# A two-layer convolution and scan network: the front of layer 0 in a planned order, with part of a depthwise convolution on VectorE

## The chip, the core and the metric

The kernel runs on one core of one Trainium2 chip, in one launch. The core has TensorE (PE in the profile), VectorE (DVE), ScalarE (ACT), GpSimd (POOL) and SyncE (SP); each takes its instructions in its own order, and they meet at semaphores. SP issues nearly all DMAs. The metric is the device time of one execution, in microseconds; lower is better. "Before" is given as the median of three runs.

## The reference

The input is an image of 64 x 64 tokens with 96 channels (L = 4096 tokens). Two layers follow each other, each with a mixer and a small network per token, both added to the residual. The change is in layer 0's mixer alone, cut here to what it touches:

```python
# x: (1, 64, 64, 96); D_INNER = 192, D_STATE = 16, DT_RANK = 6
x = (x - mean(x)) / sqrt(var(x) + 1e-6)              # over the 96 channels
xz = x @ in_proj_w
x_val, z = xz[..., :192], xz[..., 192:]
x_val = silu(depthwise_conv3x3(x_val, conv_w) + conv_b)
s1 = x_val in row order;  s3 = x_val in column order
y = scan(s1) + reversed scan(s1) + scan(s3) + reversed scan(s3)
y = layernorm(y) * silu(z)
return y @ out_proj_w

def scan(u):
    x_dbl = u @ x_proj_w                              # dt, B, C
    dt = softplus(x_dbl[:, :6] @ dt_proj_w + dt_proj_b)
    log_dA = dt * A;  dB_u = dt * B * u
    decay = exp(cumsum(log_dA))
    h = decay * cumsum(dB_u / (decay + 1e-12))
    return sum(h * C) + u * D_skip
```

In layer 0 a scan is alive only near its start: the sums of dt soon make `decay` vanish against 1e-12. So the kernel computes the four scans on their first TE = 160 tokens (the "ends"), adds these to `4 * D_skip * u`, and tests at run time whether anything further on could matter. With this data nothing does.

## The kernel before, in words

All of this lies in `front0` (L417), which ends at a branch at L309, `tc.If(self.alive > 0)`, behind which the full scan stands; it isn't taken. Then come `decays` (eight small loads on SP, L1881 and L1884) and `middle` (L1098), the rest of layer 0 and layer 1, whose order a planner lays out; the first of its instructions on TensorE is L1356.

Tokens are cut into NCH = 8 chunks of CH = 512 (8 image rows each). Channels 0 to 127 are "group 0", channels 128 to 191 "group 1". Images with a border of zeros are kept in `pad`: `pad[0][:, 0]` is the upper half of group 0, `pad[0][:, 1]` its lower half with the two halves of the 128 partitions exchanged, `pad[1]` group 1, once on each half of the partitions. So 64 x 64 diagonal weights, `self.diag` (made on POOL, L385), on the four quadrants of TensorE can take four parts of a depthwise convolution side by side. All diag products are float32.

- `norm_in0` (L440) runs a loop of NCH + 2 rounds in three stages: a chunk's mean and centring on VectorE and square on ScalarE; in the next round the variance, the root on ScalarE, the scaling and four transposes to `xt`; in the round after that the two products of the projection, which go to `pad[0]` by ScalarE (L505) and to `pad[1]` by VectorE (L506). `awake` puts products of the identity with itself between them, 26 at first. Two "edge" rows (L477) are the rows next to the middle line, wanted by the other half.
- After it `prepare0` (two Exps and a Silu on ScalarE) and `mlp_weights` twice: loads on SP and casts on VectorE, the second set in the same memory as the first.
- `conv_ends` (L518) computes the convolution at the ends of the four scans alone, first in row order (o = 0, two turns of 27 products), then in column order (o = 1, 54 and 36); `silu_ends` (L558) puts them into `ue`.
- `x_proj`, `dt_proj`, `log1p` and what follows in `scan_ends` (L688) compute the ends' scans, nearly all on VectorE, with Sigmoid, Exp and the like on ScalarE. `alive` (L855) is their run-time test.
- Beside these runs the list `beside`, one step at each call of `others`: 54 steps of the whole convolution (`conv0`, L589), four products each in four quadrants, with a Silu per finished tile (L608) and its store to `u_d` (SP), and then four steps of the gate silu(z) (`gate0`, L652), whose results go over `pad`. `scaled` (L672) multiplies by 4 D_skip on ScalarE. `add_ends` (L867) adds the ends to `y` on VectorE.

Every instruction here is wrapped in `keep`, so engines run them in the order of the program. `values_load` (L862) has each engine read `alive` before it branches.

`Order` (L141) is the planner of the later stages: operations are added with an engine, a cost, what they read and write, and buffers from named slots; `run` takes the operation that can start first by these costs, of those that can start at once the one with the longest chain behind it plus its `lead`, and emits it:

```python
od.add("DVE", cost, emit, r=[what it reads], w=[what it writes], new={key: slot tag})
```

Of the kernel before, what the change touches and what calls it, by code (L numbers as in the profile page):

```python
# [123 lines left out]
PAIRS = HW // 2  # L124

# [130 lines left out]
class Net:  # L256
    def __init__(self, ctx, tc, x, out):
# [8 lines left out]
        for c in range(NCH):  # L266
            nc.sync.dma_start(self.res[:, c], xv[:, c])
# [149 lines left out]
    def front0(self, wp, w, w1, pad):  # L417
# [5 lines left out]
        with ExitStack() as ctx:  # L423
# [6 lines left out]
            self.norm_in0(wp, lp, pm, pe, xt, pad)  # L430
# [7 lines left out]
            self.add_ends(*self.scan_ends(ep, pm, pe, pad, beside))  # L438

    def norm_in0(self, wp, lp, pm, pe, xt, pad):  # L440

        nc, keep = self.nc, self.keep
        xc, v, t = {}, {}, {}

        def small(name, c):
            return lp.tile([P, 4], F32, tag=name, name=f"{name}a{c}")

        def wide(name, c):
            return lp.tile([P, 4, CD], F32, tag=name, name=f"{name}a{c}")
# [3 lines left out]


        keep(nc.scalar.activation(small("lnr", "x")[:, 0:1], self.eps6, AF.Sqrt))

        warm = pm.tile([P, CH], F32, tag="m", name="warm")

        def awake(products):
            for _ in range(products):  # L460
                keep(nc.tensor.matmul(warm[:, 0:P], self.ident, self.ident, start=True, stop=True))

        awake(26)
        for i in range(NCH + 2):
            new, mid, old = (c if 0 <= c < NCH else None for c in (i, i - 1, i - 2))
            if old is not None:
                t[old] = [pm.tile([P, CH], F32, tag="m", name=f"in0{old}{g}") for g in range(2)]
                for g in range(2):
                    w = self.w_in[:, g * P : (g + 1) * P] if g or old < NCH // 2 else self.w_turned
                    keep(nc.tensor.matmul(t[old][g], w, xt[:, chunk(old)], start=True, stop=True))  # L470
                half = old - NCH // 2 + 1
                if half in (0, 1):

                    edge = pm.tile([P, CH], F32, tag="m", name=f"edge{half}")[:, 0:HW]
                    at = L // 2 - HW * (1 - half)
                    w = self.w_in[:, 0:P] if half else self.w_turned
                    keep(nc.tensor.matmul(edge, w, xt[:, at : at + HW], start=True, stop=True))  # L477
                awake(2 if half not in (0, 1) else 1)
            if mid is not None:
                sq, v[mid] = v[mid], small("lnv", mid)  # L480
                keep(nc.vector.tensor_reduce(v[mid], sq, AX.X, ALU.add))
                keep(nc.scalar.activation(v[mid], v[mid], AF.Sqrt, bias=self.eps6, scale=1.0 / CD))
            if new is not None:
                m, x = small("lnm", new), self.res[:, new]
                keep(nc.vector.tensor_reduce(m, x, AX.X, ALU.add))
                xc[new] = wide("lnxc", new)
                keep(nc.vector.scalar_tensor_tensor(xc[new], spread(m), -1.0 / CD, x, ALU.mult, ALU.add))
                v[new] = wide("lnsq", new)
                keep(nc.scalar.activation(v[new], xc[new], AF.Square))
            if mid is not None:  # L490
                r, xn = small("lnr", mid), wide("lnxn", mid)
                keep(nc.vector.reciprocal(r, v.pop(mid)))
# [3 lines left out]
                for j in range(4):  # L496
                    keep(nc.tensor.transpose(t4[0:CD, j, :], xn[:, j, :], self.ident))
# [11 lines left out]
            if mid is not None:  # L509
                keep(nc.scalar.copy(xt[:, chunk(mid)], tr[0:CD]))  # L510
# [2054 lines left out]
```

## Time and profile before

| | us |
|---|---|
| median of three runs | 1261.97 (1258.34 to 1267.21) |
| the profiled execution, its own time | 1267.05 |
| its span, first to last instruction | 1265.2 |
| norm and projection, until the last L506 ends | 0 to 40.1 |
| products of the ends (L537), first and last | 39.8 to 55.0 |
| first polynomial step on VectorE (L986) | 60.2 |
| last product of conv0 (L639) ends, about | 106.4 |
| `alive` written (L855) | 109.0 |
| first TensorE work behind the branch (L1356) | 122.25 |

The mean granted TensorE clock was 0.871 of full speed over the span. In the stretches that matter:

```profile
core 0: us, PE busy (x) PEld busy (x) DVE busy (x) ACT busy (x) POOL busy (x), PEclk, DMA share, GB/s
0.00:10.00 10.00, 8.24 (x48) 8.25 (x49) 5.07 (x14) 2.72 (x5) 3.37 (x34) 1.00 0.64 185
10.00:40.00 30.00, 28.43 (x149) 19.30 (x149) 19.54 (x41) 14.01 (x30) 7.27 (x15) 1.00 0.08 17
40.00:60.00 20.00, 20.00 (x330) 15.15 (x326) 4.76 (x19) 8.56 (x20) 0.00 (x0) 1.00 0.08 20
60.00:109.00 49.00, 49.00 (x432) 16.81 (x424) 47.09 (x66) 26.99 (x31) 0.00 (x0) 1.00 0.46 135
109.00:122.20 13.20, 9.57 (x30) 2.86 (x28) 3.62 (x17) 8.35 (x12) 0.00 (x0) 0.93 0.19 38
122.20:130.00 7.80, 7.75 (x14) 2.83 (x14) 1.27 (x3) 0.51 (x1) 0.41 (x3) 0.67 0.84 193
```

Each row is a stretch, then its length, then the busy time of the engines in the order PE, PEld (TensorE's weight loads), DVE, ACT, POOL, with the number of instructions; at the end the granted TensorE clock, the busy share of the DMA engines and what they moved. A float32 product leaves two records in the trace. In other lines of the timeline the first number is the start, the second the time from the first to the last of merged instructions, and brackets give the idle time before and what ended it.

### The profile page before, as it was taken

The numbers are of one execution on the slowest core, as the hardware profiler recorded it, in microseconds if no ns is written. First come the engines' busy times: TensorE is split into PE (matmuls) and PEld (weight loads), VectorE is DVE, ScalarE is ACT, GpSimd is POOL, SyncE is SP. The second block draws the span as 40 slices with busy tenths as digits, with TensorE's granted clock in tenths as the row PEclk, the third lists the DMA queues.
The fourth block names the chain that finished last, engine by engine and source line by source line (L and its number), as shares of the span: only waits on it lengthen the run. The fifth ranks groups of instructions, "written<-read, shape, count | busy, mean of one in ns | idle before, by whom it ended". The sixth has DMA issues, their size and how long they took to land.

```text
span 1265.2 us, 11505 instructions
## 1 busy us (share of the span) xinstructions
PE 1042.1 (82%) x3666; PEld 427.2 (34%) x3666; DVE 1138.5 (90%) x922; ACT 884.0 (70%) x1068; POOL 847.7 (67%) x517
## 2 busy tenths in 40 slices
PE   9998988987367788897778877787778889898886
PEld 7632233322122222332222222333223444333434
DVE  6395698577989999999999999999999999999787
ACT  4455566545677878888778877888778878777435
POOL 3000385243277878978888878988888878976566
PEclk9999989997578888888878889898789999888875
DMA  2062110146755665545735675545736766423201
GB/s 74 13 171 77 26 26 13 50 152 209 232 172 158 224 219 196 149 137 178 243 126 157 224 209 206 148 139 175 239 126 196 241 210 222 149 80 93 78 1 51
DMA packets 79134, 183.17 MB, mean 145 GB/s; under 512 B 21534, under 2 KB 34936, under 8 KB 77688
## 3 DMA queue, kind: packets, MB, share of 16 engines
q1 hardware_dynamic: 78376, 182.16, 45.7%
q8 instruction: 31, 0.51, 0.2%
q14 instruction: 39, 0.32, 0.1%
q10 hardware_dynamic: 688, 0.19, 0.1%
HBM read 159.73 MB, written 21.52 MB: 143 GB/s over the span
## 4 chain that ended last, share of the span: by engine, by line
DVE 41%; PE 15%; issue 9%; ACT 4%; DMA 2%; POOL 1%; SPq 0%; another core or an unknown queue 0%; POOLq 0%; DVEq 0%; ACTq 0%
DVE xws L2007 13%; DVE h1s L2007 12%; DVE h0s L2007 7%; PE hs L2018 6%; PE hs L2022 3%; DVE x1s L2007 3%; DVE x0s L2007 2%; DVE x2s L2007 2%; ACT da L1992 2%; ACT xws L1977 1%; DMA kept<-xn 1%; PE acc L2046 1%; POOL hss L2012 1%; DMA x2s<-bc 1%; PE late L2332 1%
## 5 line engine op out<-in xcount | busy, mean ns | idle before, releaser
L2035 POOL TENSOR_TENSOR kept<-kept,kept 128x1024 f32<-128x1024 f32 x92 | 216.9, 2358 | 81.9 <-issue 39.8
L2012 POOL TENSOR_TENSOR hss<-h1s,xws 128x1024 f32<-128x1024 f32 x96 | 228.1, 2378 | 60.0 <-DVE xws L2007 57.2
L2018 PE MATMUL hs<-h0s,ident 128*128 128x512 f32 x360 | 220.1, 697 | 28.0 <-DVE h0s L2007 24.1
L1992 ACT ACTIVATE da<-dt1s,a 128x1024 f32<-128x1024 f32 x168 | 187.5, 1117 | 69.3 <-DVE xws L2007 54.7
L2007 DVE TENSOR_TENSOR_SCAN xws<-da,xws 128x1024 f32<-128x1024 f32 x96 | 222.1, 2313 | 12.4 <-ACT da L1992 12.3
L1992 ACT ACTIVATE da<-dt0s,a 128x1024 f32<-128x1024 f32 x166 | 185.1, 1116 | 39.7 <-DVE h0s L2007 16.1
L2022 PE MATMUL hs<-hss,ident 128*128 128x512 f32 x368 | 189.1, 606 | 21.4 <-POOL hss L2012 21.4
L2007 DVE TENSOR_TENSOR_SCAN h1s<-da,h1s,xws 128x1024 f32<-128x1024 f32 x72 | 167.6, 2328 | 0.8 <-ACT da L1992 0.5
L2046 PE MATMUL acc<-kept,fold 128*32 128x512 f32 x368 | 88.7, 694 | 68.5 <-POOL kept L2035 68.5
L2031 ACT COPY kept<-hs 128x512 f32<-128x512 f32 x184 | 107.1, 582 | 48.5 <-PE hs L2022 47.7
L2018 PEld LDWEIGHTS hs<-h0s,ident 128*128 128x128 f32 x360 | 71.3, 215 | 152.8 <-issue 82.3
L2022 PEld LDWEIGHTS hs<-hss,ident 128*128 128x128 f32 x368 | 69.4, 193 | 120.6 <-issue 78.8
L2018 PE MATMUL hs<-x0s,ident 128*128 128x512 f32 x128 | 73.5, 658 | 13.8 <-DVE x0s L2007 13.8
L2018 PE MATMUL hs<-x1s,ident 128*128 128x512 f32 x128 | 72.4, 650 | 13.4 <-DVE x1s L2007 13.4
L1971 POOL TENSOR_TENSOR x1s<-x1s,dus 128x1024 f32<-128x1024 f32 x32 | 75.5, 2361 | 8.8 <-DMA x1s<-bc 8.8
L2018 PE MATMUL hs<-x2s,ident 128*128 128x512 f32 x120 | 67.5, 646 | 14.5 <-DVE x2s L2007 14.5
L1971 POOL TENSOR_TENSOR x2s<-x2s,dus 128x1024 f32<-128x1024 f32 x32 | 75.8, 2367 | 0.3 <-DMA x2s<-bc 0.3
L2007 DVE TENSOR_TENSOR_SCAN x0s<-da,x0s 128x1024 f32<-128x1024 f32 x32 | 74.0, 2313 | 1.1 <-ACT da L1992 1.1
L2007 DVE TENSOR_TENSOR_SCAN x1s<-da,x1s 128x1024 f32<-128x1024 f32 x32 | 74.0, 2313 | 1.1 <-ACT da L1992 1.1
L2007 DVE TENSOR_TENSOR_SCAN x2s<-da,x2s 128x1024 f32<-128x1024 f32 x32 | 74.1, 2316 | 0.9 <-ACT da L1992 0.7
L1244 POOL MEMSET pairs<- 96x256 f32 x1 | 0.3, 308 | 103.3 <-ACTq L309 103.3
L1977 ACT COPY xws<-x1s 128x1024 f32<-128x1024 f32 x32 | 63.4, 1980 | 5.2 <-POOL hss L2012 5.2
(372 smaller groups left out, 1973.7 us busy)
## 6 DMA issues: line engine op xcount, KB each, us to landing
kept<-bc SPq DMA_DIRECT2D x92, 512.0 KB
x2s<-bc SPq DMA_DIRECT2D x32, 512.0 KB
x0s<-bc SPq DMA_DIRECT2D x28, 512.0 KB
x1s<-bc SPq DMA_DIRECT2D x28, 512.0 KB
dus<-du SPq DMA_DIRECT2D x20, 512.0 KB
dt1s<-dt SPq DMA_DIRECT2D x20, 512.0 KB
dt0s<-dt SPq DMA_DIRECT2D x20, 512.0 KB
kept<-xn SPq DMA_DIRECT2D x24, 384.0 KB
```

The source lines that it names most:

```text
L1244: nc.gpsimd.memset(self.pairs1[:, :, 0 : HW + 2 : HW + 1, :], 0.0)
L1971: keep(nc.gpsimd.tensor_tensor(x, x, du[:, part[j]], ALU.mult))
L1977: keep(copy(grid(xw)[:, w, :], cols(xs[i % 3])[:, w, :]))
L1992: keep(nc.scalar.activation(t, dts[o][:, part[j]], AF.Exp, scale=self.a6[:, g, k : k + 1]))
L2007: keep(nc.vector.tensor_tensor_scan(to, da, x, start, ALU.mult, ALU.add))
L2012: keep(nc.gpsimd.tensor_tensor(cols(hs)[:, w, :], grid(h1)[:, w, :], grid(xw)[:, w, :], ALU.add))
L2018: keep(nc.tensor.matmul(t, self.ident, x[:, chunk(m)], start=k == 0, stop=False))
L2022: keep(nc.tensor.matmul(sums[i, m], self.ident, hs[:, chunk(m)], start=False, stop=True))
L2031: keep(nc.scalar.copy(to, sums.pop((i, j * (SC // CH) + h))))
L2035: keep(nc.gpsimd.tensor_tensor(t, t, times_c_by(i, a), ALU.mult))
L2046: keep(nc.tensor.matmul(to, self.fold4, src, start=k == 0, stop=k == NK - 1))
L2332: keep(nc.tensor.matmul(at["s", a, h], self.ident, t[:, s], start=k == 0, stop=k == 1))
```

## The change

- `norm_in0` is laid out by the planner instead of the three-stage loop. Chunks come in the order 0, 7, 1, ..., 6, and SP loads them in this order. Mean and variance come from VectorE's statistics instruction (two per chunk); the Square on ScalarE and two reductions go. Both copies to `pad` are ScalarE's. Of the products that fill TensorE only the first 26 are left.
- The row-order ends (`conv_ends` with o = 0, tap by tap, and their `silu_ends`) are planned into it too, as soon as chunks 0 and 7 are in `pad`. In the program `silu_ends` then stands ahead of `prepare0`.
- The upper half of group 0 (half of the tokens of 128 channels) leaves TensorE: `upper_tap` computes it on VectorE, in two parts of 16 rows by 64, nine taps each, the first a product with a scalar per channel, the other eight in place: multiply and add. ScalarE's Silu then works in place on `y`.
- `conv0` has 36 steps instead of 54: each is four products, one per quadrant, the lower half of group 0 with group 1. The calls of `others` are moved accordingly, `scaled(0)` is called after 27 steps and the last two gate steps before `yc`.
- `x_proj` scales with ScalarE instead of VectorE.
- 14 products of the identity are put in front of `yc` (L860).

```diff
@@ -122,6 +122,8 @@
+IN_DVE, OTHERS = (), (15, 9, 9)
 BY_SUMS, TIMES_POOL = (0, 1), (0, 3)
@@ -263,7 +265,7 @@
         xv = x.rearrange("(c p j) d -> p c j d", c=NCH, j=4)
-        for c in range(NCH):
+        for c in (0, NCH - 1, *range(1, NCH - 1)):
             nc.sync.dma_start(self.res[:, c], xv[:, c])
@@ -427,7 +429,8 @@
             xt = fp.tile([CD, L], F32, tag="xt", name="xt0")
-            self.norm_in0(wp, lp, pm, pe, xt, pad)
+            ue = ep.tile([P, 6, TW], F32, tag="ue", name="ue")
+            self.norm_in0(wp, lp, pm, pe, xt, pad, ue)
             self.prepare0()
@@ -435,87 +438,103 @@
             beside = self.conv0(pm, pad) + self.gate0(pm, xt)
-            self.add_ends(*self.scan_ends(ep, pm, pe, pad, beside))
-    def norm_in0(self, wp, lp, pm, pe, xt, pad):
+            self.add_ends(*self.scan_ends(ep, pm, pe, pad, ue, beside))
+    def norm_in0(self, wp, lp, pm, pe, xt, pad, ue):
         nc, keep = self.nc, self.keep
-        xc, v, t = {}, {}, {}
...
+        od = Order()
+        at, act, dve = od.at, nc.scalar, nc.vector
+        for tag, n, shape in (("st", 4, [P, 4, 3]), ("sd", 4, [P, 4]), ("xn", 3, [P, 4, CD])):
+            od.slots(tag, [lp.tile(shape, F32, tag=f"{tag}{k}", name=f"{tag}a{k}") for k in range(n)])
+        banks = [pm.tile([P, CH], F32, tag="m", name=f"in0{k}") for k in range(3)]
+        od.slots("m", banks)
+        od.slots("e", [pe.tile([P, CH], F32, tag="e", name=f"tr0{k}") for k in range(2)])
+        keep(act.activation(lp.tile([P, 1], F32, tag="rt", name="rt"), self.eps6, AF.Sqrt))
+        for _ in range(26):
+            keep(nc.tensor.matmul(banks[0][:, 0:P], self.ident, self.ident, start=True, stop=True))
         def spread(t):
...
+        def product(key, w, where):
+            return lambda: keep(nc.tensor.matmul(at[key][:, 0 : where.stop - where.start], w, xt[:, where], start=True, stop=True))
+        def normal(c):
+            x, st, sd, xn, tr = self.res[:, c], ("st", c), ("sd", c), ("xn", c), ("tr", c)
+            def stats():
+                for k in range(2):
+                    to = at[st].rearrange("p j s -> p (j s)")[:, 6 * k : 6 * k + 6]
+                    keep(dve.bn_stats(to, x[:, 2 * k : 2 * k + 2].rearrange("p j d -> p d j")))
+            def turned():
+                t4 = at[tr].rearrange("c (p j) -> c j p", j=4)
                 for j in range(4):
-                    keep(nc.tensor.transpose(t4[0:CD, j, :], xn[:, j, :], self.ident))
...
+                    keep(nc.tensor.transpose(t4[0:CD, j, :], at[xn][:, j, :], self.ident))
+            od.add("DVE", 0.7, stats, r=[("res", c)], new={st: "st"})
+            od.add("ACT", 0.3, lambda: keep(act.activation(at[sd], at[st][:, :, 2], AF.Sqrt, bias=self.eps6, scale=1.0 / CD)), r=[st], new={sd: "sd"})
+            od.add("DVE", 0.17, lambda: keep(dve.reciprocal(at[sd], at[sd])), w=[sd])
+            od.add("DVE", 0.67, lambda: keep(dve.tensor_tensor(at[xn], x, spread(at[st][:, :, 1]), ALU.subtract)), r=[("res", c), st], new={xn: "xn"})
+            od.add("DVE", 0.56, lambda: keep(dve.tensor_tensor(at[xn], at[xn], spread(at[sd]), ALU.mult, saturate=False)), r=[sd], w=[xn])
+            od.add("PE", 0.65, turned, r=[xn], new={tr: "e"})
+            od.add("ACT", 0.58, lambda: keep(act.copy(xt[:, chunk(c)], at[tr][0:CD])), r=[tr], w=[("xt", c)])
+        def projected(c):
+            k, row = divmod(c, NCH // 2)
+            to = [pad[0][:, k, 1 + row * ROWS : 1 + (row + 1) * ROWS, 1 : HW + 1], pad[1][:, 1 + c * ROWS : 1 + (c + 1) * ROWS, 1 : HW + 1]]
+            for g in range(2):
+                key = ("in", c, g)
+                od.add("PE", 0.88, product(key, self.w_in[:, g * P : (g + 1) * P] if g or not k else self.w_turned, chunk(c)), r=[("xt", c)], new={key: "m"})
+                e, f, cost = (("ACT", act.copy, 0.58), ("DVE", dve.tensor_copy, 0.69))[g and c in IN_DVE]
+                od.add(e, cost, lambda f=f, g=g, key=key: keep(f(to[g], grid(at[key]))), r=[key], w=[("pad", c, g)])
+            half = c - NCH // 2 + 1
+            if half in (0, 1):
+                key, start = ("edge", c), L // 2 - HW * (1 - half)
+                od.add("PE", 0.2, product(key, self.w_in[:, 0:P] if half else self.w_turned, slice(start, start + HW)), r=[("xt", c)], new={key: "m"})
+                row = pad[0][:, 1 - half, half * (HW // 2 + 1), 1 : HW + 1]
+                od.add("DVE", 0.15, lambda key=key: keep(dve.tensor_copy(row, at[key][:, 0:HW])), r=[key], w=[key])
+        order = (0, NCH - 1, *range(1, NCH - 1))
+        for c in order:
+            od.add("SP", 0.0, lambda: None, w=[("res", c)], kb=192)
+        for n, c in enumerate(order):
+            od.lead = 100.0 - 10.0 * n
+            normal(c)
+            projected(c)
+        od.lead = -100.0
+        od.add("POOL", 6.0, lambda: self.diagonals(wp), w=["diag"])
+        ends = [("pad", c, g) for c in (0, NCH - 1) for g in range(2)]
+        for turn in range(2):
+            for tap in range(9):
+                od.add("PE", 0.38, lambda turn=turn, tap=tap: self.conv_ends(pm, ue, pad, 0, turn, (tap,)), r=[*ends, "diag"], w=["ends"])
+        od.add("ACT", 2.2, lambda: self.silu_ends(ue, 0), r=["ends"], w=["ue"])
+        for h in range(2):
+            rows = [("pad", c, 0) for c in range(2 * h, 2 * h + 3 - h)] + [("edge", NCH // 2)] * h
+            for tap in range(9):
+                od.add("DVE", 1.13, lambda h=h, tap=tap: self.upper_tap(pad, h, tap), r=rows, w=[("upper", h)])
+        od.run()
+    def upper_tap(self, pad, h, tap):
+        nc, keep = self.nc, self.keep
+        dy, dx = divmod(tap, 3)
+        n = 2 * ROWS
+        v = pad[0][:, 0, h * n + dy : h * n + dy + n, dx : dx + HW]
+        to = grid(self.y[0][:, h * n * HW : (h + 1) * n * HW])
+        w = self.cw[0][:, tap : tap + 1]
+        if tap:
+            keep(nc.vector.scalar_tensor_tensor(to, v, w, to, ALU.mult, ALU.add))
+        else:
+            keep(nc.vector.tensor_scalar(to, v, w, None, ALU.mult))
     def image(self, pad, g, rows, c, tap):
         return pad[g][rows, c * ROWS + dy : c * ROWS + dy + ROWS, dx : dx + HW]
-    def conv_ends(self, pm, ue, pad, o, turn):
+    def conv_ends(self, pm, ue, pad, o, turn, taps=range(9)):
@@ -524,11 +543,11 @@
         self.pad0_0, self.pad1_0 = pad
-        if turn == 0:
+        if turn == 0 and taps[0] == 0:
             self.ends = [pm.tile([P, TW], F32, tag="m", name=f"ec{o}{k}") for k in range(3)]
         t = self.ends
-        for tap in range(9):
+        for tap in taps:
             dy, dx = divmod(tap, 3)
@@ -605,49 +624,26 @@
             to = self.y[g][:, chunk(n)]
-            keep(nc.scalar.activation(to, tiles.pop((g, n)), AF.Silu, bias=self.vec[g][:, 0:1]))
+            keep(nc.scalar.activation(to, tiles.pop((g, n), to), AF.Silu, bias=self.vec[g][:, 0:1]))
             for r, c in at:
                 nc.sync.dma_start(self.u_d[g][:, chunk(c)], to[r])
-        def wide(c0, turn, tap):
+        def taps(i, tap):
             def f():
                 dy, dx = divmod(tap, 3)
+                at = slice(i * ROWS + dy, i * ROWS + dy + ROWS)
                 for k, r in enumerate(LANES):
-                    c = c0 + (k + turn) % 2
...
+                    v = self.image(pad, 1, r, i // 2 * 4 + i % 2 + 2 * k, tap)
+                    keep(nc.tensor.matmul(tile(0, half + i)[LANES[1 - k]], self.diag[2][r, tap], pad[0][r, 1, at, dx : dx + HW], start=tap == 0, stop=tap == 8))
+                    keep(nc.tensor.matmul(tile(1, i)[r], self.diag[1][r, tap], v, start=tap == 0, stop=tap == 8))
+                if tap == 8:
+                    for c in (half + i, i):
                         finish(0, c, [(slice(0, P), c)])
+                    finish(1, i, [(to, i // 2 * 4 + i % 2 + 2 * h) for h, to in enumerate(LANES)])
             return f
-        def narrow(s0, tap):
...
+        return [taps(i, tap) for i in range(half) for tap in range(9)]
     def gate0(self, pm, xt):
@@ -685,7 +681,7 @@
             keep(nc.tensor.matmul(t[:, j, :], y[1][r, at[1]], w[1][r], start=False, stop=True))
-    def scan_ends(self, ep, pm, ps, pad, beside):
+    def scan_ends(self, ep, pm, ps, pad, ue, beside):
@@ -717,7 +713,7 @@
             )
-        ue, xe = tile6("ue", TW), ep.tile([XW, 4, TE], F32, tag="xe", name="xe")
+        xe = ep.tile([XW, 4, TE], F32, tag="xe", name="xe")
         z, dt = tile6("ze"), tile6("dte")
@@ -728,7 +724,7 @@
             keep(nc.tensor.matmul(t[0:XW, 0:TE], self.w_x[1][r], ue[r, 4 + d // 2, 0:TE], start=False, stop=True))
-            keep(nc.vector.tensor_scalar(xe[:, d, :], t[0:XW, 0:TE], self.gain[0:XW], None, ALU.mult))
+            keep(nc.scalar.activation(xe[:, d, :], t[0:XW, 0:TE], AF.Copy, scale=self.gain[0:XW]))
         def dt_proj(j):
@@ -753,9 +749,6 @@
             self.polynomial(z[:, s, :], zz[:, s, :], dt[:, s, :], p[:, s, :], keep)
-        for turn in range(2):
-            self.conv_ends(pm, ue, pad, 0, turn)
-        self.silu_ends(ue, 0)
         self.conv_ends(pm, ue, pad, 1, 0)
@@ -811,7 +804,7 @@
                 )
-        others(15)
+        others(OTHERS[0])
         keep(nc.scalar.activation(w, v, AF.Sigmoid, bias=self.lneps))
@@ -829,12 +822,12 @@
         keep(nc.vector.tensor_tensor(v, v, bc[1], ALU.mult))
-        others(9)
+        others(OTHERS[1])
         t = ps.tile([P, CH], F32, tag="e", name="leastt")
         keep(nc.tensor.matmul(t[0:1, 0:P], one, self.ident, start=True, stop=True))
-        others(18)
         self.scaled(0)
-        others(9 + 1)
+        others(OTHERS[2])
+        others(1)
         self.scaled(1)
@@ -855,10 +848,13 @@
         x = x[:, :, 0:TE]
+        others(2)
+        warm = ps.tile([P, CH], F32, tag="e", name="warm")
+        for _ in range(14):
+            keep(nc.tensor.matmul(warm[:, 0:P], self.ident, self.ident, start=True, stop=True))
         yc = [pm.tile([P, TE], F32, tag="m", name=f"yc{w}") for w in range(2)]
             keep(nc.tensor.matmul(t, self.dup[r], x[r, 5], start=True, stop=True))
-        others(2)
         self.alive = nc.values_load(
```

## The prediction

> **What bounds the kernel now.** I read the page first: VectorE is 90% busy over the span and the chain of waits is VectorE scans of layer 1. None of that is touched. The change lies wholly before the branch at L309, so the second view is the timeline of 0 to 123 us, in order of time, and the third the waits and branch events around its end.
>
> ```profile
> span 1265.2 us, 11505 instructions
> ...
> DVE 41%; PE 15%; issue 9%; ACT 4%; DMA 2%; POOL 1%; SPq 0%; another core or an unknown queue 0%; POOLq 0%; DVEq 0%; ACTq 0%
> ```
>
> ```profile
> 1.75 8.95 PE L461 MATMUL warm<-ident 128*128 128x128 f32 x52 [1.75 <-POOL ident masks.py:199]
> ...
> 39.45 0.69 DVE L506 COPY pad<-in 128x512 f32<-128x512 f32 x1 [2.85 <-PE in L470]
> ...
> 46.31 1.47 ACT L577 ACTIVATE ue<-ec,vec 128x192 f32<-128x192 f32 x4 [3.99 <-PE ec L537]
> ...
> 60.21 0.33 DVE L986 TENSOR_SCALAR w<-v 128x320 f32<-128x320 f32 x1 [0.24 <-ACT v L749]
> ...
> 108.89 0.14 DVE L855 TENSOR_SCALAR alive<-low 1x1 int32<-1x1 f32 x1
> ...
> 118.62 0.60 ACT L666 ACTIVATE pad<-z 128x512 f32<-128x512 f32 x1 [0.42 <-PE z L664]
> ...
> 122.25 1.22 PE L1356 MATMUL bank<-y,mean 128*128 128x512 f32 x1 [3.68 <-ACTq L309]
> ```
>
> The reader sees four stretches. Until 39.8 the norm and input projection run chunk by chunk, every 3.54 us (an L506 copy starts at 32.37, 35.91 and 39.45). From 39.8 to 60.2 the ends of the depthwise convolution go through TensorE and ScalarE while VectorE waits. From 60.2 to 109 VectorE is the bound: its waits in that window are these two alone.
>
> ```profile
> DVE v L830 <- ACT v L828: 0.6, 1, 0.6
> DVE w L986 <- ACT v L749: 0.2, 1, 0.2
> ```
>
> After 109.0 VectorE is nearly done, but TensorE finished the convolution only at 106.3, and the four gate steps (2.9 us each) keep ScalarE until 119.2. The events of L862 and L309 show what then holds the rest of the program:
>
> ```profile
> L862 DVEq TENSOR_LOAD <-alive x1: 545/545/545, 114.1 to 114.1; - x1
> ...
> L862 ACTq TENSOR_LOAD <-alive x1: 463/463/463, 118.6 to 118.6; - x1
> ...
> L309 DVEq EVENT_SEMAPHORE  x1: 21/21/21, 117.6 to 117.6; - x1
> ...
> L309 ACTq EVENT_SEMAPHORE  x1: 17/17/17, 122.2 to 122.2; - x1
> ```
>
> Each engine passes the branch about 3 us after its last work; PE, POOL and SP all wait for the last, ScalarE. What the front loses or gains before that point moves the rest as a block.
>
> **The norm.** Removed: per chunk, two reductions, the Square on ScalarE, the lock-step loop and 36 of the 62 filler products. New VectorE work per chunk: two statistics (L2397, the same form on 192 elements, 0.35 each), reciprocal 0.17, subtract and multiply 0.56 each (L493): 1.99, times 8, plus two edge copies 0.44: 16.4 us. ScalarE takes both image copies: 0.30 + 0.58 + 2 x 0.58 = 2.0 per chunk. TensorE: four transposes 0.45 (start to next start), two products 1.83: 2.28 per chunk, 18.2 for eight, edges about 1.0, and the 54 products of the first ends, moved in here, 6.3 (39.8 to about 46.1). The first 26 fillers stay and occupy TensorE until 10.54, whatever VectorE does: bound 10.54 + 18.2 + 1.0 + 6.3 = 36.0. I add 2 us for bubbles (the first product waits for the ScalarE copy of the first transposes, about 1.0, the second 0.6): first ends done at 38.0 instead of 46.1, a gain of **8.1**. The gaps lie between 0 and 4, by the wait for one such copy or one at each of four chunks.
>
> **The second ends and the chain to VectorE.** L537 for the other scan order, projections, and ScalarE work keep their lengths, so the first polynomial, at 60.21, could start at 52.1. The scale of x_proj moves from VectorE to ScalarE: two copies of about 0.4 (L731, 0.38) are queued there behind the Sigmoid and Square of the first dt_proj, which end at 60.18 in old time, where VectorE did the last at 59.98. The second dt_proj then starts about 0.95 late, and its Square, now ending at 63.24 just in time for VectorE at 63.27, is late: **+0.95**. The first two copies find ScalarE idle. silu_ends inside the norm brings one more table load (1.28, L399's) and prepare0 comes after it: 38.2 + 1.3 + 1.5 + 3.1 = 44.1, before ScalarE's next need at 47. SP's loads for L776 wait with xe, another us; they land before their first use at 77.8 (old time), 9 us after the last broadcast was issued for the first and more for the second.
>
> **The taps.** 18 new VectorE instructions on 128x1024. No two-input tap is in the trace. Nearest: L988 0.49 for 320 and L1727 0.685 for 512 elements of the same operation give 1.0 ns per element, hence 1.20; L1626, two inputs of 1024, took 1.22. I take 1.22 for 16 and 0.69 for the two first taps (L1724, 0.42 for 512): 20.9 us. The lower end is 1.13 each; the upper is the row of the scan, 2.3, below as a rival. VectorE starts at 4.1, does three chunks by 10.6, then each third-next chunk waits for transposes to free its buffer; with TensorE's pace that puts the last norm at about 22.3, the taps' end at 43.5. Behind them are the weight casts with their reload: 40.06 to 47.09 now, 7.0 us, so 50.5. That is before 52.1, so the taps cost **nothing**, covered by the ends on TensorE and ScalarE, with a margin of only 1.6 us. Each further 0.1 us per tap costs 1.8, less the margin. I charge 0.3 for that closeness.
>
> **The middle of the front.** From the first polynomial to `alive` VectorE's work is unchanged, 48.8 us. The 0.6 wait at L830 should go: 18 of 36 steps (0.86 each, four quadrants in either version) end at about 68, then three Silus (1.8), two table loads (1.28 each), Sigmoid (3.4) and Exp (3.3) end at 79, just when L829 ends. Gain **0.6**. So `alive` at 109.0 - 8.1 + 0.95 - 0.6 + 0.3 = 101.6.
>
> **The end.** conv0 falls from 54 to 36 steps: 15.5 us less on TensorE. It ends near 84, the gates near 96, ScalarE by 98 with both d4 scalings before them: this no longer holds the branch. What is late next is VectorE: its 16 additions take 0.55 + 1.74 + 1.51, no longer stopped by L676 (2.4), and its branch signal came 2.4 us after their end: `alive` + 6.3. TensorE needs about 4.4 after `alive`, ScalarE 3.7. So L1356 starts at 107.9 instead of 122.25: **-14.3 us** (7.4 up to `alive`, 6.9 behind it: 13.2 becomes 6.3).
>
> After it SP has the six loads of L1881 and L1884 (115.4 to 119.95 now, until it waits for ScalarE): SP passes its own branch at about `alive` + 3.5 and ends them near 110, some 2 us behind TensorE instead of in step. At L1401 SP waited 4.5 us for ScalarE, so this is covered; without that wait it would cost the 2 us.
>
> **A rule against the trace.** L1356's weight loads are 0.85 apart from 123.3 to 125.8 and 0.43 at 129.1: the stage behind the branch starts at half clock, after 3.7 us without work. The 14 new filler products aim at this. The Trainium skill, "TensorE: Matmul & The Clock Gate", Part 1: The HAM clock gate, says that about 3.4 us of idleness suffices to halve the clock. Between yc at 101.5 and L1356 at 107.9 lie 6 us. By the rule the fillers buy nothing there, by their intent some 3 us (-17). I take zero: the cold start stays as the row has it. Themselves they cost 28 records of 0.12, 3.4 us, from 96 on: beside VectorE.
>
> **The sum.** The profiled execution took 1267.05 (span 1265.2 and 1.85 around it): 1252.75. It stands 0.4% above the median of 1261.97; scaled, **1248**, or 1.1% less.
>
> **The rivals.** *Forecast, 62%:* -11.5 to -17 us, 1245 to 1250.5.
> *VectorE or TensorE falls behind in the norm, 21%:* the order was laid out as if TensorE were free at the start, but it is not before 10.5, so VectorE, which goes strictly in order, may stand at full buffers longer. For: the margin of 1.6 and three xn buffers. Against: 2.28 per chunk on TensorE against 1.99. Four to eight us given back: 1252 to 1256.
> *More, 9%:* no bubbles, and the clock held: -17 to -20: 1242 to 1245.
> *Slower or nothing, 8%:* one mechanism: a tap with two reads and an in-place result at the rate of L2007's scan, 2.3 us for 1024. Eighteen cost 41.4 instead of 20.9, with the casts VectorE is free only at 71, 19 us after 52, `alive` comes at 119 and L1356 at 125.5: +3.3, 1265. It decides from 2.1 us per tap on (L1356 back at 122.25 means `alive` at 116, the first polynomial at 67.7, the taps' end at 60.7, 38 us for 18). Against it: L988 and L1727.
>
> **Numbers.** About 1% (12.6 us) is what a measurement of this kernel can tell from no change; the forecast is barely beyond it. Faster by over 1% is under 1249.4: most of the forecast (0.54) and the better case, with the runs' spread of 9 us, 0.63. Slower over 1% takes more than the last rival's row gives (2.8 us per tap): 0.03. The remaining 0.34 is within 1%. Range 1241 to 1256: the forecast, the better case and nearly all of the second, widened by 1 to 2 us for runs.
>
> **What would show it.** Right: first ends' Silu near 38, the last tap before 45 at 1.2 us each, the first polynomial near 52, `alive` near 101.6, L1356 near 108 with VectorE's signal last at L309, L1356's first loads still 0.85 apart. Wrong: VectorE waiting for nothing but its own taps before L986; ScalarE or TensorE still last at the branch; an equal front with a later start of L2007 in the middle.

## The result, and the profile after

The changed kernel took 1250.3 us in the median (1247.22 to 1252.9, five runs), beside 1263.5 us for the kernel before (1258.34 to 1267.21, five runs): a ratio of 0.9898, interval 0.9872 to 0.9925. A second set of runs of the same kernel, among the experiments below, gave 1246.84 us and 0.9893 (0.9871 to 0.9916). So it is about 1% faster. The profiled execution took 1247.49 us instead of 1267.05; that difference, 19.6 us, is larger than that of the medians (13.2) because the profiled execution of before lies at the upper end of its runs and that of after near the lower end.

First the head of the page and the chain of waits after the change:

```profile
span 1245.7 us, 11134 instructions
...
DVE 42%; PE 14%; issue 9%; ACT 6%; DMA 3%; POOL 0%; another core or an unknown queue 0%; POOLq 0%; DVEq 0%; SPq 0%; ACTq 0%
```

The chain is still VectorE's, as before, and the program has 371 instructions fewer. Where the front went is in the timeline of after, the same landmarks as before the change (start, time, engine and line, tiles, and in brackets the wait):

```profile
9.65 0.60 PE L475 MATMUL tr<-ident,xna 128*96 128x128 f32 x4
...
24.18 19.22 DVE L529 SCALAR_TENSOR_TENSOR y<-pad,cw,y 128x1024 f32<-128x1024 f32 x16
...
35.77 1.47 ACT L596 ACTIVATE ue<-ec,vec 128x192 f32<-128x192 f32 x4 [3.81 <-PE ec L556]
...
49.76 0.21 DVE L2467 CAST b<-b2q 128x96 f32<-128x96 fp8e5 x1
...
49.88 0.32 DVE L982 TENSOR_SCALAR w<-v 128x320 f32<-128x320 f32 x1
...
98.44 0.13 DVE L848 TENSOR_SCALAR alive<-low 1x1 int32<-1x1 f32 x1
...
104.51 4.73 PE L1352 MATMUL bank<-y,mean 128*128 128x512 f32 x6 [5.68 <-DVEq L311]
```

Two separate gains are to be seen. `alive` is written at 98.44 instead of 108.89: 10.5 us, all but 0.1 of it won ahead of the first polynomial step (49.88 instead of 60.21). And from `alive` to the first TensorE work behind the branch it is 6.07 us instead of 13.36: another 7.3. Together 17.7 us. The bracket of the last line names VectorE's branch signal, where ScalarE's stood before. The events at the branch, after, by source line (duration in ns, then first and last start):

```profile
L311 PEldq COMPARE_BRANCH  x1: 3640/3640/3640, 99.2 to 99.2; - x1
L311 DVEq COMPARE_BRANCH  x1: 72/72/72, 101.5 to 101.5; - x1
L311 ACTq EVENT_SEMAPHORE  x1: 17/17/17, 102.2 to 102.2; - x1
...
L311 PEldq EVENT_SEMAPHORE  x1: 51/51/51, 102.9 to 102.9; - x1
L311 DVEq EVENT_SEMAPHORE  x1: 21/21/21, 104.3 to 104.3; - x1
```

ScalarE is at its branch at 99.1 and has passed at 102.2; in the kernel before that was 122.2. The last to arrive is VectorE, which has 15 additions left behind `alive`, reads it at 100.8 and is at its branch at 101.5.

### The profile page after: what moved, and what is told of

Same layout as the page of the kernel before. It is cut to its first block, busy times and chain, and to the rows that moved or that the text cites. A ratio compares the mean times of both kernels' runs of the same rounds, so it can differ in the third digit from the quotient of the medians.

```text
span 1245.7 us, 11134 instructions
## 1 busy us (share of the span) xinstructions
PE 1025.0 (82%) x3478; PEld 417.4 (34%) x3478; DVE 1146.2 (92%) x928; ACT 886.1 (71%) x1073; POOL 849.4 (68%) x517
## 4 chain that ended last, share of the span: by engine, by line
DVE 42%; PE 14%; issue 9%; ACT 6%; DMA 3%; POOL 0%; another core or an unknown queue 0%; POOLq 0%; DVEq 0%; SPq 0%; ACTq 0%
DVE h1s L2003 13%; DVE xws L2003 12%; DVE h0s L2003 7%; PE hs L2014 6%; DVE x2s L2003 3%; PE hs L2018 3%; DVE x1s L2003 3%; ACT da L1988 2%; DMA kept<-xn 2%; ACT xws L1973 2%; DVE x0s L2003 2%; PE acc L2042 1%; DMA dt<-hss 1%; DVE x0s L2401 1%; PE late L2310 1%
## 5 line engine op out<-in xcount | busy, mean ns | idle before, releaser
L2014 PE MATMUL hs<-h0s,ident 128*128 128x512 f32 x360 | 223.3, 706 | 28.7 <-DVE h0s L2003 24.2
L2014 PE MATMUL hs<-x0s,ident 128*128 128x512 f32 x128 | 75.1, 672 | 13.2 <-DVE x0s L2003 13.2
L2014 PE MATMUL hs<-x1s,ident 128*128 128x512 f32 x128 | 74.8, 670 | 12.2 <-DVE x1s L2003 12.2
L2014 PE MATMUL hs<-x2s,ident 128*128 128x512 f32 x120 | 70.2, 670 | 14.6 <-DVE x2s L2003 14.6
L1967 POOL TENSOR_TENSOR x0s<-x0s,dus 128x1024 f32<-128x1024 f32 x28 | 66.4, 2371 | 0.0
```

Source lines behind the costliest of these rows:

```text
L1967: keep(nc.gpsimd.tensor_tensor(x, x, du[:, part[j]], ALU.mult))
L2014: keep(nc.tensor.matmul(t, self.ident, x[:, chunk(m)], start=k == 0, stop=False))
```

## The experiments

The profiles give four marks for each kernel, in us from the start: the first ends' Silu, the first polynomial step, `alive`, and the first TensorE work behind the branch. Ratios are to the kernel before on the same chip as the run, with a 95% interval; they are estimated from the single runs and are not the quotient of the medians shown.

| kernel | first Silu | polynomial | `alive` | behind the branch | median | ratio |
|---|---|---|---|---|---|---|
| before | 46.31 | 60.21 | 108.89 | 122.25 | 1263.5 | 1 |
| before, once more | 45.82 | 59.70 | 108.38 | 121.67 | 1263.76 | 1.0007 (0.9991 to 1.0024) |
| after | 35.77 | 49.88 | 98.44 | 104.51 | 1250.3 | 0.9898 (0.9872 to 0.9925) |
| after, once more | 36.34 | 50.19 | 98.97 | 105.10 | 1246.84 | 0.9893 (0.9871 to 0.9916) |
| norm alone | 35.73 | 49.59 | 98.54 | 115.60 | 1258.07 | 0.9973 (0.9958 to 0.9989) |
| taps alone | 45.70 | 66.21 | 114.47 | 123.16 | 1266.1 | 1.0034 (1.0014 to 1.0054) |
| x_proj's scale on VectorE | 36.38 | 57.85 | 106.59 | 112.65 | 1261.67 | 1.0000 (0.9980 to 1.0020) |
| without the 14 fillers | 35.97 | 49.84 | 98.58 | 104.69 | 1247.56 | 0.9892 (0.9871 to 0.9913) |
| casts on GpSimd | 35.70 | 49.55 | 98.35 | 104.47 | 1246.75 | 0.9892 (0.9871 to 0.9912) |
| 8 first fillers, not 26 | 34.78 | 48.86 | 98.79 | 105.22 | 1248.31 | 0.9889 (0.9864 to 0.9914) |
| both of these | 35.14 | 48.99 | 97.78 | 103.90 | 1248.26 | 0.9897 (0.9878 to 0.9915) |
| two idle steps before `alive` | 36.17 | 50.03 | 106.91 | 112.92 | 1254.65 | 0.9951 (0.9927 to 0.9974) |
| four idle steps before `alive` | 36.53 | 50.42 | 117.10 | 122.42 | 1262.5 | 0.9999 (0.9979 to 1.0018) |

**The two kernels once more.** No edit; a second profile of each.

> The changed kernel once more, as a control and for a second profile. If the front is fixed and only what follows the branch varies, L1352 starts at 104.5 us within 0.3 again, and the total is 1247 to 1254; if the front varies too, L1352 moves by more than 1 us. Last scan and end of the span show how much of the spread lies behind the branch.

> The kernel before once more, for a second profile of it. First TensorE work behind the branch near 122 again if the profile shown is a typical one for the front. What lies behind the branch in it: 1143 us in the profile shown, while 1262 less 1.85 less 122.3 leaves 1138 for the median; theory: the front is fixed and the rest varies by some 5 us from run to run. Rival: the front itself varies by several us.

Both repeat the marks of the front within 0.6 us. That is not the whole scatter: in the profile with four idle steps, with nothing edited up to there, the granted clock is 0.57 from 52 to 56 us (1.00 in after), ScalarE's Sigmoid (L809) comes later, and VectorE waits 1.1 us for it. So a difference of less than about 1.5 us in the last two marks need not be an edit's. What lies behind the branch scatters more: from the fourth mark to the end of the span it is 1143.0 and 1144.5 us in the two profiles of before, 1141.2 and 1140.2 in those of after.

**The norm alone.** The whole convolution goes back to TensorE; the planned norm with the ends in it stays.

```diff
         # norm_in0
-        for h in range(2):
-            rows = ...
-            for tap in range(9):
-                od.add("DVE", 1.13, lambda h=h, tap=tap: self.upper_tap(pad, h, tap), r=rows, w=[("upper", h)])
         # conv0: 54 steps, as in the kernel before
         # scan_ends
+        others(18)
         self.scaled(0)
-        others(OTHERS[2])
-        others(1)
+        others(9 + 1)
         self.scaled(1)
```

> The planned norm, the moved ends, the scale on ScalarE and the 14 fillers stay; the whole convolution is on TensorE again in 54 steps. Theory (two parts that each lift another limit): the first polynomial is at 49.6 us as in the changed kernel, alive at 98, but TensorE ends conv0 only near 96 and ScalarE the last gate near 108.5, so the TensorE start behind the branch is near 111.8: 7 us later than with the taps, 10.5 earlier than before. Rival (the taps only move work, and VectorE holds the branch anyway): start at 104 to 105, equal to the changed kernel.

`alive` is at 98.54, as in the full change (98.44): all of the gain ahead of it comes from the planned norm with the ends in it. Which part of that makes it (the statistics instruction, the planner's order, the copies on ScalarE, the 36 filler products left out of the loop, or the place of the ends) no run separates. Yet the branch comes 11 us later than in the full change. The timeline of this kernel around it:

```profile
107.80 0.60 ACT L681 ACTIVATE pad<-z 128x512 f32<-128x512 f32 x1 [0.42 <-PE z L679]
...
107.69 3.39 PE L873 MATMUL warm<-ident 128*128 128x128 f32 x28
111.01 0.54 PE L876 MATMUL yc<-bce,dup 64*128 64x160 f32 x4
...
111.58 1.50 DVE L888 TENSOR_TENSOR y<-y,yc 64x64 f32<-64x64 f32 x8 [8.23 <-PE yc L876]
...
115.60 2.90 PE L1371 MATMUL bank<-y,mean 128*128 128x512 f32 x3 [4.05 <-DVEq L311]
```

The convolution on TensorE ends at 96, the gate steps behind it at 107.7. `yc` stands behind them and behind the 14 fillers, 3.4 us; VectorE waits 8.23 us for it with eight additions to do, then goes to its branch. So the same `alive` is worth 11 us less while TensorE still has 54 steps of convolution to do. The branch is 3.8 us later than was expected, because the expectation took ScalarE's end alone and left out that `yc` stands behind the gates and the fillers (3.4 + 0.5 us); in the full change neither is on the path.

**The taps alone.** The norm loop of before, the 18 taps behind it, the first ends in `scan_ends` again; the 36 steps and the rest of the change stay.

```diff
         # norm_in0: the three-stage loop of the kernel before, then
+        for tap in range(9):
+            for h in range(2):
+                self.upper_tap(pad, h, tap)
         # scan_ends
+        for turn in range(2):
+            self.conv_ends(pm, ue, pad, 0, turn)
+        self.silu_ends(ue, 0)
         self.conv_ends(pm, ue, pad, 1, 0)
```

> The loop of before with its reductions, the ends in scan_ends, but the 18 taps on VectorE behind the loop, 36 steps, the scale on ScalarE and the fillers. Theory: without the planned norm the taps have no cover; they end near 61.5 us, the casts near 68, the first polynomial is near 68 instead of 60.2, alive near 117, the start behind the branch near 122.7: no gain over before (0 to +1 us). Rival (18 steps off TensorE are a gain by themselves): the branch follows alive at 109 and the start is near 115, 7 us earlier than before.

It is slower than the kernel before by 0.34%. VectorE's timeline, and the first TensorE work behind the branch:

```profile
39.44 1.41 DVE L531 TENSOR_SCALAR y<-pad,cw 128x1024 f32<-128x1024 f32 x2
40.77 19.21 DVE L529 SCALAR_TENSOR_TENSOR y<-pad,cw,y 128x1024 f32<-128x1024 f32 x16
...
66.21 0.32 DVE L985 TENSOR_SCALAR w<-v 128x320 f32<-128x320 f32 x1
...
123.16 3.37 PE L1355 MATMUL bank<-y,mean 128*128 128x512 f32 x4 [4.35 <-DVEq L311]
```

The taps cost the same 1.20 us each as in the full change, but start at 39.4 instead of beside the norm from 21.0. Casts and polynomial come behind them; the first polynomial is 6 us later than before the change. `alive` is 5.6 us later. At the branch the relief of TensorE gives most of that back, and no more. VectorE waits 2.4 us for `yc` here, which stands behind the gate steps and the 14 fillers (TensorE's timeline):

```profile
108.60 3.78 PE L657 MATMUL z<-xt,w_in 96*128 96x512 f32 x4
...
114.22 4.12 PE L857 MATMUL warm<-ident 128*128 128x128 f32 x28
```

The same four records of a gate step take 1.98 us in the full change. From 100 to 114 us the granted clock of this execution is 0.50. If the branch followed `alive` by 6.1 us as in the full change, it would come near 120.6 (an estimate), 1.7 us ahead of before instead of 0.9 behind it; the bulk of the loss, at the first polynomial, doesn't depend on this. Norm alone wins 6.7 us at the branch, taps alone lose 0.9, both win 17.7: each part removes one of two holders of the branch, and only with both gone does it move as far as either allows.

**x_proj's scale on VectorE.** One line back.

```diff
-            keep(nc.scalar.activation(xe[:, d, :], t[0:XW, 0:TE], AF.Copy, scale=self.gain[0:XW]))
+            keep(nc.vector.tensor_scalar(xe[:, d, :], t[0:XW, 0:TE], self.gain[0:XW], None, ALU.mult))
```

> The changed kernel with the scale of x_proj back on VectorE. Theory: VectorE takes it in order, behind taps and casts that end at 49.9 us; the second projection waits for it and the first polynomial comes near 55.4, 5.5 us later than in the changed kernel, and so does the start behind the branch (110). Rival, as the prediction had it: the scale on ScalarE costs 0.95 us in the queue there, so that its return to VectorE gains up to 1 us.

In the runs it takes the whole gain away: a ratio of 1.0000. The first polynomial is 8.0 us later than in the full change. The timeline of this kernel, VectorE, then TensorE, and the stretch from 50 to 57 us:

```profile
50.44 0.67 DVE L727 TENSOR_SCALAR xe<-xe,gain 80x160 f32<-80x160 f32 x2
56.69 0.38 DVE L727 TENSOR_SCALAR xe<-xe,gain 80x160 f32<-80x160 f32 x1 [5.59 <-PE xe L726]
...
57.85 0.31 DVE L982 TENSOR_SCALAR w<-v 128x320 f32<-128x320 f32 x1
```

```profile
51.16 1.43 PE L732 MATMUL de<-xe,w_dt 6*128 6x320 f32 x2 [6.12 <-DVE xe L727]
55.73 0.50 PE L725 MATMUL xe<-ue,wx 128*80 128x160 f32 x2
```

```profile
50.00:57.00 7.00, 5.84 (x24) 1.95 (x24) 1.31 (x5) 3.26 (x5) 0.00 (x0) 0.62 0.00 0
```

The first two scalings are behind the taps and casts now, at 50.44. In the full change ScalarE does them:

```profile
41.69 0.39 ACT L727 ACTIVATE xe<-xe,gain 80x160 f32<-80x160 f32 x1 [1.30 <-PE xe L726]
42.48 0.39 ACT L727 ACTIVATE xe<-xe,gain 80x160 f32<-80x160 f32 x1 [0.41 <-PE xe L726]
```

The dt projection waits 6.12 us for them, TensorE idles, its granted clock from 50 to 57 is 0.62, and two convolution steps at that clock stand ahead of the next x_proj, whose scaling VectorE awaits for 5.59 us. In the median this kernel is 11 to 15 us behind the two sets of after, more than the 8.1 us at the branch (5.5 were expected there, without the low clock). The profiled execution (1252.34) is the fastest of its twelve, so the profile doesn't show where the rest lies: 8 us of the loss are explained, the rest is open.

**Without the 14 fillers.**

```diff
-        warm = ps.tile([P, CH], F32, tag="e", name="warm")
-        for _ in range(14):
-            keep(nc.tensor.matmul(warm[:, 0:P], self.ident, self.ident, start=True, stop=True))
```

> The changed kernel without the 14 products in front of yc. Theory (they end 6 us or more before L1352 and cannot hold the clock): L1352 starts at 104.5 to 105.1 us and its weight loads are 0.85 apart at first, both as with them; the total is equal, 1246 to 1251. Rival (they keep the clock): without them the stage behind the branch is up to 3 us longer, 1250 to 1254.

No difference: the branch at 104.69, the time within the spread of after. The first stretch of 2 us behind the branch, first this kernel's and then that of after (the last numbers are the granted clock, the DMA share and GB/s):

```profile
104.00:106.00 2.00, 1.31 (x2) 0.82 (x3) 0.00 (x0) 0.00 (x0) 0.41 (x3) 0.50 0.05 5
```

```profile
104.00:106.00 2.00, 1.49 (x2) 0.84 (x3) 0.00 (x0) 0.00 (x0) 0.41 (x3) 0.50 0.15 41
```

Half clock with the fillers as without them.

**The casts on GpSimd.** In `mlp_weights`, both casts:

```diff
-        nc.vector.tensor_copy
+        nc.gpsimd.tensor_copy
```

> The changed kernel with all casts of mlp_weights on GpSimd, which stands idle there; VectorE is then free for the first polynomial at 43.4 us instead of 49.9. Theory (VectorE and the chain over TensorE and ScalarE arrive together): the first polynomial is at 49.6 to 50.0, 0 to 0.4 us earlier, and the total is equal. Rival (VectorE with taps and casts has become the bound of this stretch): the polynomial comes 3 us or more earlier.

Nothing is won. The waits of VectorE from 42 us on, this kernel's and then those of after (total, times, longest):

```profile
DVE w L982 <- ACT v L745: 5.9, 2, 5.6
DVE v L823 <- ACT v L821: 0.3, 1, 0.3
```

```profile
DVE w1q L2463 <- DMA w1f<-w: 2.4, 1, 2.4
DVE b2q L2463 <- DMA b2f<-b: 0.9, 1, 0.9
DVE v L823 <- ACT v L821: 0.3, 1, 0.3
DVE w L982 <- ACT v L745: 0.2, 1, 0.2
```

VectorE is free at 44 and waits 5.6 us for ScalarE's Square, which releases the polynomial at 49.55; in the full change the casts end at 49.97. The two chains arrive 0.3 us apart, so making one shorter wins that and no more.

**Eight first fillers instead of 26, alone and with the casts on GpSimd.**

```diff
-        for _ in range(26):
+        for _ in range(8):
             keep(nc.tensor.matmul(banks[0][:, 0:P], self.ident, self.ident, start=True, stop=True))
```

> The changed kernel with 8 instead of 26 products of the identity at the start, so that TensorE is free at about 5 us and takes the first transposes at 7.7 instead of 9.6. Theory: the chain over TensorE gains up to 1.9 us, but VectorE has taps and casts to do and gains only what it waited for TensorE's buffers, so the first polynomial is 0.5 to 1.5 us earlier. Rival (without the products the clock is low in the norm): the norm is longer and the polynomial is not earlier, or later than 50.2.

> Both: casts on GpSimd and 8 products at the start. Theory: with VectorE free at 43, the polynomial follows the chain over TensorE and ScalarE, 1.5 to 2 us earlier than in the changed kernel (48), and L1352 with it (102.6 to 103). Rival as before: a low clock in the norm takes the gain.

In time neither is distinguishable from the change as it is. The timeline of TensorE in the first of the two, the granted clock of its stretch from 10 to 17 us, and two lines of the full change:

```profile
7.47 0.64 PE L475 MATMUL tr<-ident,xna 128*96 128x128 f32 x4 [1.94 <-DVE xna L481]
8.79 3.07 PE L462 MATMUL in<-xt,w_in 96*128 96x512 f32 x4 [0.67 <-ACT xt L483]
11.65 1.68 PE L475 MATMUL tr<-ident,xna 128*96 128x128 f32 x8
```

```profile
10.00:17.00 7.00, 6.95 (x23) 3.70 (x22) 6.56 (x18) 4.85 (x11) 6.45 (x14) 0.79 0.20 39
```

```profile
10.93 1.98 PE L462 MATMUL in<-xt,w_in 96*128 96x512 f32 x4 [0.67 <-ACT xt L483]
12.75 1.04 PE L475 MATMUL tr<-ident,xna 128*96 128x128 f32 x8
```

The first transposes start 2.2 us sooner, but the first products take 3.07 us instead of 1.98 and the next transposes 1.68 instead of 1.04, at a clock of 0.79 instead of 1.00. One of the 2.2 us is left at the first ends and at the first polynomial. At the branch the second kernel still has 0.6 of it, the first none, for it has a wait that after doesn't have:

```profile
DVE bce L822 <- ACT w L809: 1.1, 1, 1.1
```

It is the wait that the profile with four idle steps has too, behind a like drop of the clock (0.81 from 48 to 52 us, 0.76 from 52 to 56). The kernel with four idle steps has all 26 products at the start, so the loss between polynomial and `alive` is not shown to be the edit's.

**Idle steps ahead of `alive`.** The changed kernel with two or four multiplications of a tile that nothing reads any more, 4.0 us each, ahead of `alive`.

```diff
+        for _ in range(4):
+            keep(nc.vector.tensor_tensor(w, w, w, ALU.mult))
         low = ep.tile([1, 1], F32, tag="low", name="low")
```

> The kernel after with two idle multiplications of 4.0 us each (a tile that nothing reads any more, squared) on VectorE ahead of the smallest-of-the-minima reduction; they reach the branch and nothing else. Branch and first TensorE work behind it 8.0 us later, near 112.6. Theory one: what lies behind the branch does not depend on when it comes, so the time is that of after plus 8.0, near 1255.5. Theory two: the 3 us that the change won in the front and that are missing in the end come from the time at which the later work starts (the loads issued before the branch then land sooner against it), so only 6 to 7 us show, near 1254.

> As late2 with four multiplications: branch 16.1 us later, near 120.6, which is nearly where it was before the change. Theory one: after plus 16.1, near 1263.5, above the kernel before by as much as the 3 us missing. Theory two: near 1260, since a late start gives the later work back its shorter course.

With four the branch is where the kernel before has it (122.42, before 122.25), and the time is that of the kernel before: 1262.5, ratio 0.9999 (0.9979 to 1.0018). All else that the change does is still in this kernel, 18 steps less of convolution on TensorE among it. So the change works on the total through the time of the branch and, within 0.2%, through nothing else. The branch is 17.9 us later than in after instead of 16.1; the wait for ScalarE above is a part of the difference. In time 12.2 and 15.7 us of that show against the two medians of after, and by the ratios about 13. That leans to theory two, which has less than the delay come out at the end, but it does not decide: the branch is read from one execution, and single executions of one kernel spread over 9 us.

## Why the prediction was right, and where its terms were off

It said 1248 us, by 14.3 us in the front and nothing behind it. The median is 1250.3, in the range; the mechanism was the one forecast, but the front gave more than the sum said, 17.7 us, and of that only 13.2 showed in the medians. That these two misses nearly cancel, so that the number is close, is luck.

**The first ends, -8.1 predicted, -10.5 measured.** Two terms were mis-sized. The bubbles: TensorE stood idle for 1.25 us from 10 to 30 us instead of 2 (0.75). The norm's work on TensorE without the ends: about 18.5 us instead of 19.2 (0.7), most of it the two edge products, charged at 1.0, which take 0.4 here (22.66 to 23.05) and took 0.17 each in the kernel before. The remaining 0.9, the first fillers' end at 9.65 instead of 10.54, is chance and no gain of the change: in the other profiles with these 26 products TensorE goes on to its next work between 9.09 (norm alone) and 10.53 (four idle steps). "VectorE or TensorE falls behind in the norm" did not happen: from 17 to 30 us TensorE was busy for 13.00 of 13.00.

**x_proj's scale, +0.95.** The term that was read wrongly. In the full change the second polynomial waits 0.15 us for ScalarE, and ScalarE's second Square comes 3.35 us behind its first instead of 3.06: 0.3, half of it hidden. More important is what the working did not ask: what the scaling would stand behind if it stayed. On VectorE it stands behind taps and casts and costs 8 us at the first polynomial. The edit charged as a small loss is a condition of the gain.

**The taps, nothing, with a margin of 1.6.** Right in price and in sum: sixteen in 19.22 us (1.20 from start to start, 1.22 assumed; L1626, read there as 1.22, lasted 1.23 to 2.28 in the kernel before, and the taps go with the least of these), two firsts at 0.72 and 0.74 (0.69), end at 43.4 (43.5), casts until 49.97 (50.5). The margin was not there: with the ends over 2 us earlier than forecast ScalarE's Square is done at 49.60, so the casts are the later of the two by 0.3. That this is just what was charged for closeness is luck, since the charge was for a chain 2 us later. `alive` in the kernel without taps, 98.54, shows directly that they cost nothing. The slower rival, a tap at 2.3 us, falls with the 1.20; that taps can hold the front is shown by the kernel with taps alone, where they stand behind the norm.

**L823 (L830 before), -0.6.** Half right: 0.3 of the wait is left.

**From `alive` to the branch, 6.3 predicted, 6.07 measured.** Right, and by the engine named: VectorE's signal last. The gates ended at 93.9 (96 predicted). Norm alone shows what it would be with conv0 still at 54 steps.

**SP's six loads 2 us behind TensorE.** Wrong: SP issues the next stage's first load at 104.56, in step with TensorE at 104.51. In the kernel before two of the eight loads went out ahead of SP's branch and six behind it; in the changed kernel all eight go out from 85.4 to 90.7, ahead of the branch, so none was left to issue behind it.

**The clock and the 14 fillers, nothing.** Right. The rule weighed there, from the Trainium skill's "TensorE: Matmul & The Clock Gate", Part 1: The HAM clock gate, agrees with the rows. From `yc` to the first work behind the branch TensorE is idle for 5.68 us with the fillers and for 5.37 without them, longer than the 3.4 us of idleness that the page names, and the clock behind it is 0.50 either way. TensorE's own branch instruction is 3640 ns of that (99.2 to 102.9). `yc` comes behind the fillers and waits for VectorE, so they don't shorten this gap.

**The middle unchanged.** Not settled. Median less 1.85 us around the span, less the fourth mark, gives the time behind the branch. With a late branch it is 1139.4 for before (by its 1263.5), 1140.2 for its second set, 1141.1 with taps alone and 1138.2 with four idle steps; with the branch of the full change 1143.9, 1139.9 for its second set, 1141.0 without the fillers, 1140.4 with the casts on GpSimd, 1141.2 with 8 first fillers and 1142.5 with both. On average the later stages take about 2 us longer after an early branch, which would be part of what the total lacks of 17.7 us. But the profiles of the two kernels before have 1143.0 and 1144.5 there, so single executions differ by more. One source of that scatter is in the traces: the half clock behind the branch lasts from about 3 us (taps alone) to about 6 (after, once more). No experiment isolated a cause.

## What to carry to other kernels

Where several engines meet at one point, list for each the time at which it arrives, and what holds it; an edit that frees one alone is worth only the distance to the next (6.7 and -0.9 us here, 17.7 for both). When work is put on an engine that runs strictly in order, ask not only what it costs there, but which short steps of other chains now stand behind it, and move those away first: scalings of 0.4 us left behind the taps put the first polynomial 8 us back, and in the medians the whole gain was gone. What filler products ahead of real work win in clock has to be set against the time that they take (26 and 8 at the start gave the same total), and they win nothing where TensorE stands idle behind them for 5 us and more, as at this branch; there they must not stand ahead of anything that is waited for.

## What the runs showed of the hardware

The branch itself is dear, and not because of the comparison. Each engine's branch instruction lasts 45 to 72 ns on VectorE, ScalarE, GpSimd and SyncE, and then 2.4 to 3.8 us pass before its next event; on TensorE it is one record of 3.4 to 3.8 us in all thirteen profiles. There is one exception: GpSimd passes in 0.5 us (99.1 to 99.6, and 98.5 to 99.0) in the two kernels with the casts on it, over the same skipped block. From 98.5 to 104.5 us after the change only instruction queues move data:

```profile
q14 instruction: 7, 0.06, 3.1%
q8 instruction: 2, 0.03, 2.6%
```

This fits what the Trainium skill's "Runtime: NRT & Kernel Launch", Instruction fetch mechanics, says of a taken branch whose target lies outside what is already loaded, that the target page has to be fetched before execution goes on; that the fetch is all of the time, and that GpSimd needed none in the exception, no run shows. Of the 6 us from `alive` at 98.44 to 104.51, VectorE's 15 additions take the first half and its branch, 2.8 us from 101.5 to 104.3, the second.

The granted clock does not follow long idleness alone. With four idle steps and with 8 first fillers it falls to about half for some 3 us in the stretch from 50 to 56 us, where TensorE had been idle for 0.44 us only; the other profiles with the same gap have 1.00 there. With taps alone it stays at 0.50 for 14 us in which TensorE is busy throughout. The rule cited above covers neither, and no run shows what sets them off.

A two-input tap in place on VectorE, with rows of 64 out of a wider image and a scalar per partition, runs at 1.20 us for 1024 float32 elements, about half of the 2.3 us that the row of the scan (L2007 of the kernel before) gives for as many; the products with a scalar alone took 0.72 us.
